# Edge sums in PSUM, biases on DVE, one wide product and a narrower count in a three-sweep graph kernel

## The chip, the cores and the metric

The kernel runs on one core of one Trainium2 chip. The metric is the device time of the whole kernel in microseconds, measured on the chip. Five runs of the kernel before gave 4110.39 us as the median (4082.2 to 4133.68). One further execution was recorded by the hardware profiler and took 4101.04 us; all the rows quoted below are from that execution.

The engines are called PE (TensorE, matrix products), DVE (VectorE, elementwise work), ACT (ScalarE), POOL (GpSimd, which here issues the gathers) and SP (SyncE, which here issues plain transfers). SBUF is the working memory on the chip, PSUM the small memory that PE writes its products to.

## The reference

A graph has 6250 nodes with 256 features each and 100000 edges. Each edge has a source node `src`, a destination node `dst` and 64 features of its own. The edges come sorted by `dst`. Cut to what matters:

```python
# layer 0
theta_x = (x[dst] - x[src]) @ theta_w.T + theta_b
phi_x = x[src] @ phi_w.T + phi_b
x = layernorm(x + segment_max(relu(theta_x + phi_x), dst))   # 0 for a node without edges
# layer 1
hv = x @ W_in + b_in
for W, b in ((W_u0, b_u0), (W_u1, b_u1)):
    m = relu(concatenate([hv[src], edge_attr_64]) @ W + b)
    hv = where(has_in, segment_max(m, dst) + hv, hv)
out = layernorm(x + relu(hv @ W_ro + b_ro))
```

`segment_max` takes, for every node, the maximum over the edges that end in it. Three times, then, a row of 256 numbers is fetched for every edge, something is added, and a maximum is taken over all edges with the same destination.

## The kernel before, in words

**Edges.** The sorted edges lie in 17 blocks (`BLOCKS`: twelve of 56 steps, then 48, 32, 16, 8 and 6; 782 steps, `FS`). In a block each of the 128 partitions holds a contiguous run of edges, and one step handles one edge of every partition. Eight steps are a chunk (`K`), so there are 98 chunks (`NG`).

**Three sweeps** (`sweep(r)`) go over all the steps, each with its own table of node rows in HBM. The product of the node's row is computed once per node, not per edge, and written to `table[r]`. In a sweep:

- POOL gathers the rows of the step's 128 sources into the chunk's tile `run` (`sources`, L719, one indirect DMA a step, issued 16 steps ahead in the order of the program; `run` has four buffers of eight steps).
- In sweeps 1 and 2 the edge's own 64 features add a product. PE multiplies the features of two steps at once with `whe` (`pair`, L730, one 512-column product in a PSUM tile `hp`; two buffers, issued one pair ahead) and DVE adds it to two steps of `run` (L923). `features` loads the features by ACT's queue.
- DVE then takes the running maximum (L926): the new row against the previous step's row, which a per-partition limit `lim` lets through only where the destination is the same.
- After each chunk SP writes the eight rows to `S` in HBM (L932).
- At the end of a block `over_lanes` carries the maximum on from partition to partition: transposes on PE, scans on DVE, copies on ACT.

**Nodes.** The 6250 nodes are 49 tiles of 128. As soon as the blocks of a tile's edges are done, `node` gathers the last row of each node's run from `S` (L771), merges what was carried between partitions (`picks`, `carried`, a product `v`), finishes the node's row and multiplies it for the next sweep. The helper `turned` transposes on PE and copies on ACT (L694); the helper `times` (L697 to L703) multiplies by a weight, two products of 256 columns, and then adds the bias by a third product of a row of ones with the bias row (L702). In sweep 0 these are: theta on `xT` (`theta`, with ACT's copy `theta_out`, L801), and two products of the normalised row, one with a bias for `table[1]` (`first_f`, copied by `first_h`, L830) and one without for `h_sb` (`first_g`, copied by `first_i`, L834). In sweep 1 it is the product for `table[2]` (`next_c`, copied by `next_d`, L849), in sweep 2 the last product, which DVE takes together with the relu and the residual (`last_d`, L853).

**Counting.** In sweep 0 the edges of every node are counted, which yields the position of each node's last edge. Every three steps (slots 4 to 295) `count` compares, on DVE, the low seven bits of the destinations with 0 to 127 (`ol`, L647, 1024 elements for eight steps) and the high bits with 0 to 48 (`oh`, L650, 392 elements), and PE multiplies the two into the histogram `hist` (L653). No node can be finished before the counting ends, which is at step 300.

**Order.** The whole of it is under a manual schedule: each engine executes its instructions in the order in which the Python code emits them. `at(slot, f)` puts a piece of a node's work after the edge work of step `slot`, so the pieces of several nodes interleave with the steps: for a node whose first piece stands at slot b, `picks` at b-3, `carried` at b-2, then `first_a` to `first_i` at b to b+10 (`next_a` to `next_d` at b to b+5, `last_g` at b+9). Theta of tile t is at slot 8t+20 and its copy one slot later. Semaphores between the engines are set from the data dependencies, and a tile with few buffers makes its next writer wait for its last reader.

[...]

**Start.** `fuse` multiplies weights once so that `wcat` holds `W_in` beside `W_in W_u0`, and `fuse_b` folds `b_in` into the other biases, all of which are rows on one partition (`line`).

Of the kernel before, what the change touches and what calls it, by code (L numbers as in the profile page):

```python
# [23 lines left out]
K = 8  # L24
# [525 lines left out]
def in_order(ctx: ExitStack, tc: tile.TileContext, g):  # L550
# [30 lines left out]
    def line(v, name):  # L581
        t = one.tile([1, D], F32, name=name)
        nc.scalar.dma_start(t, v.rearrange("(o f) -> o f", o=1))
        return t
# [47 lines left out]
    def fuse_b():  # L632
        for b, w in ((b2, wu0), (bu1, wu1), (bro, wro)):
            ps = psum.tile([P, 512], F32, tag="pr", name="fuse_p")
            for k in range(2):
                nc.tensor.matmul(ps[:1, :D], binT[:, k:k + 1], w[:, k, :], start=(k == 0), stop=(k == 1))
            nc.vector.tensor_add(b, b, ps[:1, :D])
# [3 lines left out]
    hist = psum.tile([P, 512], F32, tag="v", name="hist")  # L641

    def count(c):
        k = min(K, FS - c * K)
        cut = slice(c * K, c * K + k)
        ol = work.tile([P, K, P], BF16, name="ol", bufs=1)
        nc.vector.tensor_tensor(ol[:, :k, :], col.unsqueeze(1).to_broadcast([P, k, P]),  # L647
                                lo[:, cut].unsqueeze(2).to_broadcast([P, k, P]), OP.is_equal)
        oh = work.tile([P, K, NT], BF16, name="oh", bufs=1)
        nc.vector.tensor_tensor(oh[:, :k, :], col[:, :NT].unsqueeze(1).to_broadcast([P, k, NT]),  # L650
                                hi[:, cut].unsqueeze(2).to_broadcast([P, k, NT]), OP.is_equal)
        for j in range(k):
            nc.tensor.matmul(hist[:, :NT], ol[:, j, :], oh[:, j, :], start=(c == 0 and j == 0),  # L653
# [43 lines left out]
    def times(aT, w, b, n, tag="pr"):  # L697
        ps = psum.tile([P, 512], F32, tag=tag, name="prod")
        for k in range(2):
            nc.tensor.matmul(ps[:, :n], aT[:, k, :], w[:, k, :], start=(k == 0), stop=(k == 1 and b is None))  # L700
        if b is not None:
            nc.tensor.matmul(ps[:, :n], every[0:1, :], b, start=False, stop=True)  # L702
        return ps  # L703

    def sweep(r):
# [21 lines left out]
        def pair(i):  # L727
            c, q = divmod(i, K // 2)
            hp[i] = psum.tile([P, 512], F32, tag="he", name="hp")
# [33 lines left out]
        def node(t, g, b):  # L763
# [22 lines left out]
            def carried():  # L786
                assert max(carried_in) - SPAN[t][0] < KEPT
                o["v"] = psum.tile([P, 512], F32, tag="v", name="v")
# [8 lines left out]
            def theta():  # L797
                o["h"] = times(o["xT"], th, tb, D, tag="he")

            def theta_out():  # L800
                nc.scalar.copy(h_sb[:, t, :], o["h"][:, :D])  # L801
# [20 lines left out]
            def first_f():  # L822
                o["g"] = times(o["aT"], wcat[:, :, D:], b2, D)

            def first_g():
                o["ps"] = times(o["aT"], wcat[:, :, :D], None, D)

            def first_h():
                new = work.tile([P, D], F32, name="new", bufs=3)
                nc.scalar.copy(new, o["g"][:, :D])  # L830
                nc.scalar.dma_start(table[1][t * P:(t + 1) * P, :], new)

            def first_i():
# [158 lines left out]
```

## Time and profile before

| | |
|---|---|
| median of 5 runs | 4110.39 us |
| the profiled execution | 4101.04 us, span 4099.2 us, 22048 instructions |
| granted TensorE clock, mean | 0.664 |
| PE busy | 2040.3 us (50%), 4957 matmuls |
| DVE busy | 2082.8 us (51%) |
| POOL busy | 2462.5 us (60%), 2499 instructions |
| ACT busy | 280.6 us (7%) |
| HBM traffic | 179 GB/s over the span |

The span falls into these stages (busy time of the engines in each, from the profile's windows):

| stage | us | PE | DVE | POOL | granted clock |
|---|---|---|---|---|---|
| sweep 0, counting (130 to 520) | 390 | 163 | 279 | 308 | 0.50 |
| sweep 0, rest of the steps (520 to 1338) | 818 | 294 | 318 | 495 | 0.55 |
| sweep 0, last nodes (1338 to 1392) | 54 | 43 | 31 | 6 | 0.84 |
| sweep 1, steps (1392 to 2675) | 1283 | 680 | 657 | 800 | 0.72 |
| sweep 1, last nodes (2675 to 2724) | 49 | 34 | 19 | 6 | 0.88 |
| sweep 2, steps (2724 to 4019) | 1295 | 706 | 701 | 797 | 0.71 |
| sweep 2, last nodes (4019 to 4099) | 80 | 59 | 41 | 7 | 0.65 |

How to read the rows of the profile: a group's row has the line of the code, the engine, the operation, what is written `<-` what is read, the count, the busy time in us and the mean in ns of one, and after the second bar the engine's idle time just before these instructions with what ended most of it. A product of two f32 operands shows as two matmul rows. The ends of matmuls are modelled in the profile, so that a matmul's result can be later than its row says; when the next instruction that needs it starts is measured. A timeline row has the start in us, the duration in us, the engine, the line and the operation, and in brackets the idle time before it and what ended that.

### The profile page before, as it was taken

Reading aid. Unit: us, or ns where it says so; the run is one execution under the profiler, and the core shown is the slowest. Engines: PE = TensorE matmul, PEld = TensorE weight load, DVE = VectorE, ACT = ScalarE, POOL = GpSimd, SP = SyncE. Lnnn points to the kernel's source line nnn. Section 1 sums busy time; section 2 is a strip of 40 time slices with the busy share of each in tenths; the row PEclk is TensorE's granted clock in tenths of the full one; section 3 lists DMA queues with packets and bytes.
Section 4 is the critical chain, followed back from the end, with each engine's and each line's share of the span. In section 5 each row is a group of like instructions: output and inputs, shape, how many; then the busy total and the mean of one; then the engine's idle time right before and its main releaser. Section 6 shows DMA issues by size and latency. Waiting matters only on the chain.

```text
span 4099.2 us, 22048 instructions
## 1 busy us (share of the span) xinstructions
PE 2040.3 (50%) x4957; PEld 916.1 (22%) x4957; DVE 2082.8 (51%) x4526; ACT 280.6 (7%) x770; POOL 2462.5 (60%) x2499
## 2 busy tenths in 40 slices
PE   5434344232324744455555555664545555455567
PEld 4222222111212311111121222231111212122224
DVE  2776633443334554464554444555556555555555
ACT  1000010000011100000000000110000000000001
POOL 3677755666664466566666655546666666565552
PEclk7555565555556866676677777886667777676766
DMA  6755545554554455565555555545656555454542
GB/s 223 242 190 192 196 155 171 171 176 162 171 168 143 148 190 195 170 216 179 192 194 181 181 178 177 176 154 192 205 178 213 193 183 192 161 190 154 174 161 94
DMA packets 237763, 735.87 MB, mean 180 GB/s; under 512 B 51880, under 2 KB 91799, under 8 KB 200375
## 3 DMA queue, kind: packets, MB, share of 16 engines
q0 software_dynamic: 119664, 326.92, 27.3%
q1 hardware_dynamic: 66096, 334.71, 21.3%
q10 hardware_dynamic: 51862, 72.75, 5.3%
q8 instruction: 42, 0.69, 0.1%
q14 instruction: 99, 0.80, 0.1%
HBM read 401.01 MB, written 333.16 MB: 179 GB/s over the span
## 4 chain that ended last, share of the span: by engine, by line
another core or an unknown queue 29%; issue 18%; PE 16%; DVE 15%; DMA 10%; POOL 10%; ACT 2%; ACTq 0%; POOLq 0%; DVEq 0%; SPq 0%
POOL run L719 9%; DMA run<-table,s_s 7%; DVE run L926 7%; DVE run L923 5%; PE hp L730 5%; PE prod L700 4%; PE prod L702 2%; PE v L790 2%; DMA S<-run 2%; PE ps L533 1%; PE tp L692 1%; POOL m L771 1%; ACT aT L694 1%; DVE oh L650 1%
## 5 line engine op out<-in xcount | busy, mean ns | idle before, releaser
L719 POOL DMA_INDIRECT run<-table,s_s x2346 | 2318.6, 988 | 1295.3 <-issue 658.8
L730 PE MATMUL hp<-whe,hT 128*128 128x512 f32 x1564 | 1058.1, 781 | 594.6 <-DVE run L923 374.3
L926 DVE SCALAR_TENSOR_TENSOR run<-run,lim 128x256 f32<-128x256 f32 x2295 | 1111.1, 484 | 241.4 <-DMA run<-table,s_s 157.9
L923 DVE TENSOR_TENSOR run<-run,hp 128x512 f32<-128x512 f32 x782 | 533.7, 682 | 844.7 <-remote 495.4
L730 PEld LDWEIGHTS hp<-whe,hT 128*128 128x128 f32 x1564 | 307.0, 233 | 1200.5 <-DVE run L923 704.2
L771 POOL DMA_INDIRECT m<-S,end_i x147 | 143.3, 975 | 297.1 <-DMA S<-run 197.1
L700 PE MATMUL prod<-wcat,aT 128*128 128x256 f32 x392 | 162.1, 555 | 267.3 <-ACT aT L694 170.7
L790 PE MATMUL v<-cs,pick 128*128 128x256 f32 (+1 forms) x468 | 197.4, 552 | 125.4 <-DVE pick L783 66.7
L692 PE MATMUL tp<-ident,h_sb 128*128 128x128 f32 x196 | 53.4, 365 | 382.8 <-DVE h_sb L841 255.6
L653 PE MATMUL hist<-oh,ol 128*128 128x49 bf16 x782 | 48.9, 217 | 251.2 <-DVE oh L650 218.4
L700 PEld LDWEIGHTS prod<-wcat,aT 128*128 128x128 f32 x392 | 96.3, 270 | 320.7 <-ACT aT L694 180.9
L790 PEld LDWEIGHTS v<-cs,pick 128*128 128x128 f32 x468 | 119.0, 279 | 203.1 <-DVE pick L783 65.6
L746 DVE TENSOR_TENSOR_SCAN cT<-lim,cT,lp 128x128 f32<-128x128 f32 x96 | 40.8, 467 | 184.6 <-PE lp L741 117.5
L692 PEld LDWEIGHTS tp<-ident,h_sb 128*128 128x128 f32 x196 | 25.2, 174 | 475.5 <-issue 317.4
L700 PE MATMUL prod<-wro,aT 128*128 128x256 f32 x196 | 85.4, 580 | 89.8 <-issue 49.4
L853 DVE SCALAR_TENSOR_TENSOR m<-prod,x_sb 128x256 f32<-128x256 f32 x49 | 20.8, 424 | 210.0 <-remote 96.7
L647 DVE TENSOR_TENSOR ol<-col,lo 128x1024 bf16<-128x1024 bf16 x98 | 119.1, 1215 | 5.6 <-remote 5.5
L837 DVE TENSOR_TENSOR m<-m,v 128x256 f32<-128x256 f32 x98 | 40.5, 413 | 155.6 <-remote 64.2
L700 PE MATMUL prod<-wu,aT 128*128 128x256 f32 x196 | 75.0, 520 | 71.7 <-issue 50.8
L653 PEld LDWEIGHTS <-ol 128*128 128x128 bf16 x782 | 42.7, 117 | 278.3 <-DVE ol L647 179.4
L741 PE MATMUL lp<-ident,run 128*128 128x128 f32 x102 | 28.5, 373 | 152.1 <-ACT lim L739 76.4
L700 PE MATMUL prod<-th,xT 128*128 128x256 f32 x196 | 97.8, 653 | 3.7 <-issue 3.7
(116 smaller groups left out, 1325.0 us busy)
## 6 DMA issues: line engine op xcount, KB each, us to landing
S<-run SPq DMA_DIRECT2D x291, 1024.0 KB
hT<-in_heT ACTq DMA_DIRECT2D x196, 256.0 KB
run<-table,s_s POOLq DMA_INDIRECT x2346
table<-new ACTq DMA_DIRECT2D x98, 128.0 KB
xg<-in_xTn SPq DMA_DIRECT2D x7, 896.0 KB
table<-g SPq DMA_DIRECT2D x7, 896.0 KB
xT<-in_xTn SPq DMA_DIRECT2D x49, 128.0 KB
x_sb<-in_xn SPq DMA_DIRECT2D x7, 896.0 KB
```

Source lines behind the costliest of these rows:

```text
L533: nc.tensor.matmul(ps[:, q * D:(q + 1) * D], xg[:, k, (i + q) * P:(i + q + 1) * P], wd[:, k, :], start=(k == 0), stop=(k == 1))
L647: nc.vector.tensor_tensor(ol[:, :k, :], col.unsqueeze(1).to_broadcast([P, k, P]), lo[:, cut].unsqueeze(2).to_broadcast([P, k, P]), OP.is_e ...
L653: nc.tensor.matmul(hist[:, :NT], ol[:, j, :], oh[:, j, :], start=(c == 0 and j == 0), stop=(c == NG - 1 and j == k - 1))
L692: nc.tensor.transpose(tp[:, k * P:(k + 1) * P], a[:, k * P:(k + 1) * P], ident)
L700: nc.tensor.matmul(ps[:, :n], aT[:, k, :], w[:, k, :], start=(k == 0), stop=(k == 1 and b is None))
L702: nc.tensor.matmul(ps[:, :n], every[0:1, :], b, start=False, stop=True)
L719: nc.gpsimd.indirect_dma_start(out=runs[s // K][:, s % K, :], out_offset=None, in_=table[r], in_offset=bass.IndirectOffsetOnAxis(ap=s_s[:, ...
L730: nc.tensor.matmul(hp[i], hT[c][:, q, :], whe[r - 1].rearrange("p s f -> p (s f)"), start=True, stop=True)
L771: i = nc.gpsimd.indirect_dma_start(out=o["m"], out_offset=None, in_=S_r[:P * (FIRST[SPAN[t][1]] + BLOCKS[SPAN[t][1]]), :], in_offset=bass. ...
L790: nc.tensor.matmul(o["v"][:, :N1], p, cs[:, blk % KEPT, :N1], start=(blk == SPAN[t][0]), stop=(blk == SPAN[t][1]))
L923: nc.vector.tensor_add(two, two, hp.pop(s // 2))
L926: nc.vector.scalar_tensor_tensor(cur, prev, lim[:, s:s + 1], cur, OP.min, OP.max)
```

## The change

Four things are changed together.

1. **Edge rows are summed in PSUM.** In sweeps 1 and 2 DVE adds two steps of `run` into the `hp` tile and leaves the sum there; the running maximum reads the row from PSUM and writes `run`. At the first step of a block, where no maximum is taken, a copy moves the row to `run`. `hp` has three buffers, and `pair` is issued two pairs ahead. In sweep 0 the maximum works on `run` as before.
2. **DVE adds the biases.** `times` has no bias product any more. The bias rows are loaded to all 128 partitions, and `fuse_b` works on all partitions. `theta_out`, `first_g`, `next_d` and `last_d` add the bias on DVE as they copy the product out of PSUM; the first three were copies on ACT, and `last_d` becomes two instructions.
3. **The wide product of pass 0 in one.** The products for `table[1]` and for `h_sb` become one of 512 columns, taken out by `first_g` at slot b+9.
4. **Counting.** ACT copies the low bits to two PSUM tiles (`low`), and `ol` is computed from there; `oh` covers only the node tiles that the chunk's block can contain. A product with zeros clears `hist` first.

The tag `he` has three buffers for these purposes, and `v` with `hist` one.

```diff
     def line(v, name):
-        t = one.tile([1, D], F32, name=name)
-        nc.scalar.dma_start(t, v.rearrange("(o f) -> o f", o=1))
+        t = one.tile([P, D], F32, name=name)
+        nc.scalar.dma_start(t, v.rearrange("(o f) -> o f", o=1).to_broadcast([P, D]))
...
-                nc.tensor.matmul(ps[:1, :D], binT[:, k:k + 1], w[:, k, :], start=(k == 0), stop=(k == 1))
-            nc.vector.tensor_add(b, b, ps[:1, :D])
+                nc.tensor.matmul(ps[:, :D], binT[:, k:k + 1].to_broadcast([P, P]), w[:, k, :], start=(k == 0),
+                                 stop=(k == 1))
+            nc.vector.tensor_add(b, b, ps[:, :D])
...
-    hist = psum.tile([P, 512], F32, tag="v", name="hist")
+    hist = psum.tile([P, 512], F32, tag="v", name="hist", bufs=1)
+
+    none = one.tile([P, NT], BF16, name="none")
+    nc.vector.memset(none, 0.0)
+    half = (NG + 1) // 2
+    low = []
+    for i in range(2):
+        low.append(psum.tile([P, 512], F32, tag="he", name="low", bufs=3))
+        n = min(half * K, FS - i * half * K)
+        nc.scalar.copy(low[i][:, :n], lo[:, i * half * K:i * half * K + n])
 
     def count(c):
...
-                                lo[:, cut].unsqueeze(2).to_broadcast([P, k, P]), OP.is_equal)
+                                low[c // half][:, c % half * K:c % half * K + k].unsqueeze(2).to_broadcast([P, k, P]), OP.is_equal)
+        b = max(i for i in range(NB) if FIRST[i] <= c * K)
+        tiles = [t for t in range(NT) if SPAN[t][0] <= b <= SPAN[t][1]]
+        t0, w = tiles[0], len(tiles)
         oh = work.tile([P, K, NT], BF16, name="oh", bufs=1)
-        nc.vector.tensor_tensor(oh[:, :k, :], col[:, :NT].unsqueeze(1).to_broadcast([P, k, NT]),
-                                hi[:, cut].unsqueeze(2).to_broadcast([P, k, NT]), OP.is_equal)
+        nc.vector.tensor_tensor(oh[:, :k, :w], col[:, t0:t0 + w].unsqueeze(1).to_broadcast([P, k, w]),
+                                hi[:, c * K:c * K + k].unsqueeze(2).to_broadcast([P, k, w]), OP.is_equal)
+        if c == 0:
+            nc.tensor.matmul(hist[:, :NT], ol[:, 0, :], none, start=True, stop=False)
         for j in range(k):
-            nc.tensor.matmul(hist[:, :NT], ol[:, j, :], oh[:, j, :], start=(c == 0 and j == 0),
+            nc.tensor.matmul(hist[:, t0:t0 + w], ol[:, j, :], oh[:, j, :w], start=False,
                              stop=(c == NG - 1 and j == k - 1))
...
-            nc.tensor.matmul(ps[:, :n], aT[:, k, :], w[:, k, :], start=(k == 0), stop=(k == 1 and b is None))
-        if b is not None:
-            nc.tensor.matmul(ps[:, :n], every[0:1, :], b, start=False, stop=True)
+            nc.tensor.matmul(ps[:, :n], aT[:, k, :], w[:, k, :], start=(k == 0), stop=(k == 1))
...
-            hp[i] = psum.tile([P, 512], F32, tag="he", name="hp")
+            hp[i] = psum.tile([P, 512], F32, tag="he", name="hp", bufs=3)
...
-                o["v"] = psum.tile([P, 512], F32, tag="v", name="v")
+                o["v"] = psum.tile([P, 512], F32, tag="v", name="v", bufs=1)
...
             def theta_out():
-                nc.scalar.copy(h_sb[:, t, :], o["h"][:, :D])
+                nc.vector.tensor_add(h_sb[:, t, :], o["h"][:, :D], tb)
...
             def first_f():
-                o["g"] = times(o["aT"], wcat[:, :, D:], b2, D)
+                o["ps"] = times(o["aT"], wcat, 2 * D)
 
             def first_g():
-                o["ps"] = times(o["aT"], wcat[:, :, :D], None, D)
-
-            def first_h():
                 new = work.tile([P, D], F32, name="new", bufs=3)
-                nc.scalar.copy(new, o["g"][:, :D])
+                nc.vector.tensor_add(new, o["ps"][:, D:], b2)
                 nc.scalar.dma_start(table[1][t * P:(t + 1) * P, :], new)
-
-            def first_i():
                 nc.scalar.copy(h_sb[:, t, :], o["ps"][:, :D])
...
             def next_d():
                 new = work.tile([P, D], F32, name="new", bufs=3)
-                nc.scalar.copy(new, o["ps"][:, :D])
+                nc.vector.tensor_add(new, o["ps"][:, :D], bu1)
...
             def last_d():
-                nc.vector.scalar_tensor_tensor(o["m"], o["ps"][:, :D], 0.0, x_sb[:, t, :], OP.max, OP.add)
+                nc.vector.tensor_add(o["m"], o["ps"][:, :D], bro)
+                nc.vector.scalar_tensor_tensor(o["m"], o["m"], 0.0, x_sb[:, t, :], OP.max, OP.add)
...
-                             (8, first_g), (9, first_h), (10, first_i)):
+                             (9, first_g)):
...
+                    pair(1)
...
-                if s % 2 == 0:
-                    if s + 2 < FS:
-                        pair(s // 2 + 1)
-                    two = runs[c][:, j:j + 2, :].rearrange("p s f -> p (s f)")
-                    nc.vector.tensor_add(two, two, hp.pop(s // 2))
+            if s % 2 == 0:
+                two = runs[c][:, j:j + 2, :].rearrange("p s f -> p (s f)")
+                if r > 0:
+                    if s + 4 < FS:
+                        pair(s // 2 + 2)
+                    sums = hp.pop(s // 2)
+                    nc.vector.tensor_add(sums, sums, two)
+                else:
+                    sums = two
             cur = runs[c][:, j, :]
+            row = sums[:, s % 2 * D:(s % 2 + 1) * D]
             if s > FIRST[blk]:
-                nc.vector.scalar_tensor_tensor(cur, prev, lim[:, s:s + 1], cur, OP.min, OP.max)
+                nc.vector.scalar_tensor_tensor(cur, prev, lim[:, s:s + 1], row, OP.min, OP.max)
+            elif r > 0:
+                nc.vector.tensor_copy(cur, row)
```

More of the change, by code (lines that the diff above doesn't have):

```diff
@@ L643, in count @@
+    none = one.tile([P, NT], BF16, name="none")
[6 more added lines that the diff above has]
+        nc.scalar.copy(low[i][:, :n], lo[:, i * half * K:i * half * K + n])
     def count(c):
         k = min(K, FS - c * K)
-        cut = slice(c * K, c * K + k)
         ol = work.tile([P, K, P], BF16, name="ol", bufs=1)
         nc.vector.tensor_tensor(ol[:, :k, :], col.unsqueeze(1).to_broadcast([P, k, P]),
-                                lo[:, cut].unsqueeze(2).to_broadcast([P, k, P]), OP.is_equal)
+                                low[c // half][:, c % half * K:c % half * K + k].unsqueeze(2).to_broadcast([P, k, P]), OP.is_equal)
+        b = max(i for i in range(NB) if FIRST[i] <= c * K)
+        tiles = [t for t in range(NT) if SPAN[t][0] <= b <= SPAN[t][1]]
+        t0, w = tiles[0], len(tiles)
@@ L695, in turned, with times @@
         return aT
-    def times(aT, w, b, n, tag="pr"):
-        ps = psum.tile([P, 512], F32, tag=tag, name="prod")
+    def times(aT, w, n, tag="pr"):
+        ps = psum.tile([P, 512], F32, tag=tag, name="prod", bufs=3 if tag == "he" else 2)
         for k in range(2):
-            nc.tensor.matmul(ps[:, :n], aT[:, k, :], w[:, k, :], start=(k == 0), stop=(k == 1 and b is None))
-        if b is not None:
-            nc.tensor.matmul(ps[:, :n], every[0:1, :], b, start=False, stop=True)
+            nc.tensor.matmul(ps[:, :n], aT[:, k, :], w[:, k, :], start=(k == 0), stop=(k == 1))
         return ps
@@ L797, in theta @@
             def theta():
-                o["h"] = times(o["xT"], th, tb, D, tag="he")
+                o["h"] = times(o["xT"], th, D, tag="he")
             def theta_out():
-                nc.scalar.copy(h_sb[:, t, :], o["h"][:, :D])
+                nc.vector.tensor_add(h_sb[:, t, :], o["h"][:, :D], tb)
             def first_a():
@@ L844, in next_c @@
             def next_c():
-                o["ps"] = times(o["aT"], wu1 if r == 1 else wro, bu1 if r == 1 else bro, D)
+                o["ps"] = times(o["aT"], wu1 if r == 1 else wro, D)
             def next_d():
                 new = work.tile([P, D], F32, name="new", bufs=3)
-                nc.scalar.copy(new, o["ps"][:, :D])
+                nc.vector.tensor_add(new, o["ps"][:, :D], bu1)
                 nc.scalar.dma_start(table[2][t * P:(t + 1) * P, :], new)
             def last_d():
-                nc.vector.scalar_tensor_tensor(o["m"], o["ps"][:, :D], 0.0, x_sb[:, t, :], OP.max, OP.add)
+                nc.vector.tensor_add(o["m"], o["ps"][:, :D], bro)
+                nc.vector.scalar_tensor_tensor(o["m"], o["m"], 0.0, x_sb[:, t, :], OP.max, OP.add)
             def last_e():
```

## The prediction

> **What bounds the kernel now.** I read the chain that ended last first, because the busy shares (PE 50%, DVE 51%, POOL 60%) name no engine.
>
> ```profile
> another core or an unknown queue 29%; issue 18%; PE 16%; DVE 15%; DMA 10%; POOL 10%; ACT 2%; ACTq 0%; POOLq 0%; DVEq 0%; SPq 0%
> ```
>
> On one core, 29% for "an unknown queue" means waits whose releaser the profile did not find. The costliest groups say where they sit:
>
> ```profile
> L719 POOL DMA_INDIRECT run<-table,s_s x2346 | 2318.6, 988 | 1295.3 <-issue 658.8
> L730 PE MATMUL hp<-whe,hT 128*128 128x512 f32 x1564 | 1058.1, 781 | 594.6 <-DVE run L923 374.3
> L926 DVE SCALAR_TENSOR_TENSOR run<-run,lim 128x256 f32<-128x256 f32 x2295 | 1111.1, 484 | 241.4 <-DMA run<-table,s_s 157.9
> L923 DVE TENSOR_TENSOR run<-run,hp 128x512 f32<-128x512 f32 x782 | 533.7, 682 | 844.7 <-remote 495.4
> ```
>
> The edge sum L923 idles 845 us, mostly on "remote". The timeline shows on what: a stretch at 1442 us, then one at 1512 us.
>
> ```profile
> 1441.62 0.69 DVE L923 TENSOR_TENSOR run<-run,hp 128x512 f32<-128x512 f32 x1 [3.88 <-remote]
> 1442.36 2.08 PE L730 MATMUL hp<-whe,hT 128*128 128x512 f32 x2 [3.53 <-issue]
> 1447.21 0.69 DVE L923 TENSOR_TENSOR run<-run,hp 128x512 f32<-128x512 f32 x1 [3.86 <-remote]
> 1447.95 2.07 PE L730 MATMUL hp<-whe,hT 128*128 128x512 f32 x2 [3.51 <-DVE run L923]
> ...
> 1512.39 1.12 PE L730 MATMUL hp<-whe,hT 128*128 128x512 f32 x2 [0.53 <-DVE run L923]
> 1513.29 0.68 DVE L923 TENSOR_TENSOR run<-run,hp 128x512 f32<-128x512 f32 x1
> 1514.03 1.12 PE L730 MATMUL hp<-whe,hT 128*128 128x512 f32 x2 [0.51 <-DVE run L923]
> 1514.93 0.68 DVE L923 TENSOR_TENSOR run<-run,hp 128x512 f32<-128x512 f32 x1
> ```
>
> At 1512 us (granted clock 1.0) a pair of steps takes 1.64 us: 0.68 for the sum and 2 x 0.48 for the maxima, DVE back to back. At 1442 us (clock 0.5) it takes 5.6 us; the matmul is drawn as 2.08 us, but its semaphore, which DVE waits for, comes 5.6 us after the one before. PE crawls there, whatever its row says. POOL starts a gather every 1.25 us, so a pair costs it 2.5 us. While PE crawls POOL gets ahead until its four run buffers are full, and stands still; then PE recovers and DVE catches up. I added POOL's idle stretches over 1 us: 199, 258 and 287 us in the three sweeps of about 1332, 1332 and 1376 us. **The time is POOL's 831 gathers a sweep (about 1050 us) plus what PE makes it stand still, plus a tail.**
>
> One stage differs: the counting, 130 to 520 us, where POOL never stops but is itself slow.
>
> ```profile
> 300.06 1.22 DVE L647 TENSOR_TENSOR ol<-col,lo 128x1024 bf16<-128x1024 bf16 x1
> 300.73 1.36 POOL L719 DMA_INDIRECT run<-table,s_s  x1 [0.30 <-issue]
> 301.19 0.56 DVE L650 TENSOR_TENSOR oh<-col,hi 128x392 bf16<-128x392 bf16 x1
> 302.40 1.09 POOL L719 DMA_INDIRECT run<-table,s_s  x1 [0.30 <-issue]
> ```
>
> Gathers that run beside L647 take 1.27 us on the mean, with DVE idle 0.945. Start to start it is 1.448 us over the stage's 269 gathers and 1.271 us in the rest of sweep 0.
>
> **The change, part by part**, against the profiled execution: 4101.0 us, span 4099.2, 9 us under the median of 4110.4.
>
> *Counting.* `ol` keeps one SBUF input; `oh` shrinks from 392 elements to 8 times a few tiles, some 40: 0.19 us by the 0.17 us of the 17-element L617, for 0.56. If the second SBUF input is what holds POOL up, its step falls to the 1.28 us of the rest of the sweep, where L926 still has two: 269 x 0.17 = **-45 us**. Bounds: 0, if it is not the input, and 269 x (1.448 - 1.25) = -53. Next late would be DVE: per 8 steps 2.67 x (1.22 + 0.19) + 8 x 0.52 + 0.41 for the moved theta add = 8.3 us, plus a wait for theta's product. In that stage the ACT copy followed its step's maximum by 2.2 to 3.2 us; without the bias's 1.07 us that is 1.1 to 2.1, in one of three cases under other DVE work, so 1.25 on average: 9.6 us against POOL's 10.2. Hidden, with 0.6 us to spare.
>
> [...]
>
> *Edge sums in PSUM.* The sum writes where it read; the maximum reads a PSUM row. Rows: L806, a maximum with a PSUM input and a pointer scalar, takes 484 ns, as L926 does now; 0. Bounds 1530 x (424 - 484) = -92 us of DVE by L853 (an immediate scalar), and +92 the other way; DVE is 51% busy, so little of either shows. 34 copies at block starts, 0.4 us each, lie beside POOL. One SBUF input less on these 1530 maxima: the 1562 gathers of sweeps 1 and 2 average 0.97 against 0.945 us, so at most 1562 x 0.025 = -39; I take **-25**. The third `hp` buffer lets PE run two pairs ahead, but a crawling PE is short of speed, not of work: bounds 0 and the 118 us that L923 waits for PE by name; I take **-10**.
>
> [...]
>
> *Bias matmuls gone.* 196 products lose one; each is two rows of 128x256. At 618 us six such rows (`wcat`, then `b`) kept the consumer waiting from 618.04 to 626.71, 1.44 us a row; drawn rows are 0.5 to 0.7. In sweep 0 a node has some 21 rows (4 + 2 for theta, 8 + 2 for the wide product, 3 for `v`, the rest transposes), of which 4 go: 19% of the 184 us that POOL stood still after the counting (199 less 15 at 110 us): **-35**, and -5 in the tail. In sweeps 1 and 2, 98 of some 2100 rows of 256 columns go in each, 4.6%. Pairs over 3.4 us hold 1552 of the 2573 us of these sweeps; 4.6% of that is 71 us of crawling, of which between a third (the part in which POOL stood still) and all counts: 24 to 71, taken **-40**. The bounds for all bias terms: 0, if POOL's stalls have another cause, and -120.
>
> *Wide product of pass 0.* Four rows of 512 columns for eight of 256: the same columns, 4 weight loads less, overlapped: 0, bounds ±10.
>
> *Work moved from ACT to DVE*: 147 adds of 0.41 us, 49 more in `last_d`: 80 us, in DVE's idle half: **+10**. The price is in the order: theta_out, first_g and next_d now make DVE wait for PE, with the chain of maxima behind them, and POOL waits for that through the run buffers; `table<-new` on ACT's queue then waits for DVE. Sweep 2 already has this wait (L853, 210 us idle) and its 782 steps took 1295 us against 1283 in sweep 1, so in sweep 1 at most 12, taken **+5**. In sweep 0 after the counting 13 theta adds and 49 first_g are in question:
>
> ```profile
> 623.06 1.91 PE L700 MATMUL prod<-th,xT 128*128 128x256 f32 x4
> ...
> 647.71 0.37 ACT L801 COPY h_sb<-prod 128x256 f32<-128x256 f32 x1 [20.63 <-remote]
> ...
> 649.16 0.16 DVE L805 TENSOR_SCALAR no<-v 128x1 f32<-128x1 f32 x1 [32.58 <-remote]
> ```
>
> Here theta's consumer was 24 us late, but DVE stood on the same PE queue until 649 anyway. I take **+15**; bounds 0 and the 200 us of the first rival.
>
> *Start and single buffers.* fuse_b loads 128 columns for 1, six bias lines become 128 rows each, and DVE already waits there 32 us for L637: **+5**, bounds 0 and +15. `v` keeps one buffer: the next node's matmul waits for this node's first_a, which comes two steps earlier in the order while `hp` holds PE as tightly; 0, up to +20 in the tails.
>
> Sum: -45 - 25 - 10 - 35 - 5 - 40 + 10 + 5 + 15 + 5 = -125; 4101 - 125 = 3976, said as **3980 us**, 3% below the median shown. [...]
>
> **Rivals.** *DVE becomes the place where everything waits* (slower). ACT idled 258 us before L830 and, by the timeline, some 143 us between step and L801 after the counting. If half of these 400 us becomes waiting that DVE did not have, 200 us, less the -45, -25 and -25 of counting, ports and half the bias: 4101 + 105 = 4205. It decides once an added wait outlasts POOL's lead, some 24 steps or 30 us, or if PE also crawls in the counting. For it: theta sits one step before its consumer. Against: L853 in sweep 2. *The ports do not matter*: the -45 and -25 fail, PE's gains are eaten by the waits: about 4090, no change. *PE stops crawling*: with less node work and two pairs queued, half of POOL's 545 us of idling in sweeps 1 and 2 goes as well: about 3710. Against: in a crawl PE already has two pairs queued.
>
> **Numbers.** Forecast (3880 to 4065) 0.60, larger gain 0.10, no change 0.13, slower 0.17. About 1% either way is what a measurement of this kernel can tell from no change. Faster 0.70, same 0.13, slower 0.17. The range takes most of the slower rival and part of the larger gain: 3800 to 4190.
>
> **What would show it.** Gathers in the counting start 1.25 to 1.3 us apart, not 1.45; those beside L926 fall to 0.95 us in sweeps 1 and 2 and not in sweep 0. Maxima stay near 0.48 us. The bias rows (202 us of PE by L702) are gone, POOL's idle sum falls from 744 to about 650 us. I am wrong if DVE's waits for `prod` in sweep 0 push POOL's idling past 200 us, or if crawling takes another share of the time than now: nothing in the profile fixes that share.

## The result, and the profile after

The changed kernel takes 4092.5 us (median of 42 runs, 4054.5 to 4133.4) against 4101.3 us for the kernel before (79 runs, 4055.9 to 4146.5). The ratio, which leaves out the runs more than 1.5% above the fastest of their kernel, is 0.9987, with a 95% interval of 0.9972 to 1.0002: no change that a measurement can tell. Its profiled execution took 4080.6 us, with a span of 4078.5.

The work did shrink where the change cuts it. GpSimd's (POOL) busy time fell from 2462.5 to 2381.9 us and TensorE's (PE) from 2040 to 1788.5. The time of a sweep is taken here from its first gather to the first gather of the next one, of sweep 2 to the end; "standing still" is the sum of the gaps over 1 us between two gathers of the sweep, those from `S` for the node tiles included; a "step" is the mean from one start of a gather to the next, over the gathers that follow within 2.2 us. In the counting, "time lost" is what 240 steps took beyond 240 times the mean step.

| | before | after |
|---|---|---|
| sweep 0: time, standing still | 1332, 199 us | **1373, 290 us** |
| sweep 1: time, step, standing still | 1332, 1.275, 258 us | 1306, 1.253, 253 us |
| sweep 2: time, step, standing still | 1376, 1.273, 287 us | 1340, 1.252, 281 us |
| gather for step 300 issued (end of the counting) | 505.1 us | **562.4 us** |
| counting, steps 60 to 300: step, time lost beside it | 1.450, 1 us | **1.286, 96 us** |

Sweeps 1 and 2 gained 61 us together in these two executions. The profiled executions of two later runs, `theta_act` and `bits_sbuf`, have the same code in these sweeps and make it 42 and 28, so the gain is real but smaller than one pair of profiles says. Sweep 0 lost 40, and it lost them in the counting, the stage from which the forecast took its largest term. There the step fell as forecast, and yet the stage got longer, since GpSimd now stops ten times in it.

The page of the changed kernel, its chain and its costliest groups (busy us, mean ns of one | idle before, and what ended most of it):

```profile
issue 25%; DVE 24%; another core or an unknown queue 22%; PE 13%; POOL 7%; DMA 5%; ACT 1%; ACTq 0%; DVEq 0%; POOLq 0%; SPq 0%
...
L731 POOL DMA_INDIRECT run<-table,s_s x2346 | 2240.2, 955 | 1368.6 <-issue 715.6
...
L934 DVE TENSOR_TENSOR hp<-hp,run 128x512 f32<-128x512 f32 x782 | 543.2, 695 | 487.6 <-remote 218.9
L940 DVE SCALAR_TENSOR_TENSOR run<-run,lim,hp 128x256 f32<-128x256 f32 x1530 | 733.2, 479 | 46.5 <-issue 0.2
...
L940 DVE SCALAR_TENSOR_TENSOR run<-run,lim 128x256 f32<-128x256 f32 x765 | 369.4, 483 | 153.6 <-issue 63.8
...
L656 DVE TENSOR_TENSOR ol<-col,low 128x1024 bf16<-128x1024 bf16 x98 | 118.9, 1213 | 150.8 <-remote 149.3
```

A gather is 955 ns for 988, and a maximum with a PSUM row costs 479 ns, no more than the SBUF form's 483. The chain still names no engine; "an unknown queue" is now 22%. The granted clock does not tell the kernels apart: its mean is 0.673 for 0.664 before. The last row is the new one: the compare `ol` idled 5.6 us in the kernel before and 150.8 now. Its waits in the stage, VectorE (DVE) only (engine, line, waited for: us in all, times, longest), first in the kernel before from 60 to 500 us, then in the changed one from 60 to 560 us:

```profile
DVE ol L647 <- remote: 5.5, 4, 2.5
```

```profile
DVE ol L656 <- remote: 134.7, 20, 14.4
```

What it waits for shows in the timeline of the changed kernel (start us, us, engine, line, operation, [idle before, released by]):

```profile
167.28 1.52 DVE L940 SCALAR_TENSOR_TENSOR run<-run,lim 128x256 f32<-128x256 f32 x3
...
167.43 0.35 PE L667 MATMUL hist<-oh,ol 128*128 128x3 bf16 x8 [3.75 <-DVE oh L662]
...
173.67 0.95 POOL L731 DMA_INDIRECT run<-table,s_s  x1 [0.30 <-issue]
174.92 0.94 POOL L731 DMA_INDIRECT run<-table,s_s  x1 [0.30 <-issue]
176.08 1.22 DVE L656 TENSOR_TENSOR ol<-col,low 128x1024 bf16<-128x1024 bf16 x1 [7.29 <-remote]
```

`ol` has one buffer, so the next compare waits until the eight tiny products of the last one have read it. By their rows these end at 167.8; the compare starts at 176.08, 8.3 us later, while POOL issues a gather every 1.25 us and gets ahead. At 183.6 it has run out of buffers and stands still for 14 us.

### The profile page after: what moved, and what is told of

Read it like the earlier page. It is cut to its first block, busy times and chain, and to the rows that moved or that the text cites. A ratio compares the mean times of both kernels' runs of the same rounds, so it can differ in the third digit from the quotient of the medians.

```text
span 4078.5 us, 21055 instructions
## 1 busy us (share of the span) xinstructions
PE 1788.5 (44%) x4370; PEld 763.3 (19%) x4370; DVE 2128.1 (52%) x4757; ACT 229.6 (6%) x625; POOL 2381.9 (58%) x2499
## 3 DMA queue, kind: packets, MB, share of 16 engines
q0 software_dynamic: 119664, 326.92, 27.5%
## 4 chain that ended last, share of the span: by engine, by line
issue 25%; DVE 24%; another core or an unknown queue 22%; PE 13%; POOL 7%; DMA 5%; ACT 1%; ACTq 0%; DVEq 0%; POOLq 0%; SPq 0%
DVE run L940 11%; DVE hp L934 8%; POOL run L731 6%; PE hp L742 5%; PE prod L714 5%; DMA run<-table,s_s 4%; PE v L802 1%; PE tp L706 1%; DMA S<-run 1%; DVE st L692 1%; DVE pick L795 1%; POOL m L783 1%; ACT aT L708 1%; DVE ol L656 0%
## 5 line engine op out<-in xcount | busy, mean ns | idle before, releaser
L731 POOL DMA_INDIRECT run<-table,s_s x2346 | 2240.2, 955 | 1368.6 <-issue 715.6
L934 DVE TENSOR_TENSOR hp<-hp,run 128x512 f32<-128x512 f32 x782 | 543.2, 695 | 487.6 <-remote 218.9
L940 DVE SCALAR_TENSOR_TENSOR run<-run,lim,hp 128x256 f32<-128x256 f32 x1530 | 733.2, 479 | 46.5 <-issue 0.2
L940 DVE SCALAR_TENSOR_TENSOR run<-run,lim 128x256 f32<-128x256 f32 x765 | 369.4, 483 | 153.6 <-issue 63.8
L656 DVE TENSOR_TENSOR ol<-col,low 128x1024 bf16<-128x1024 bf16 x98 | 118.9, 1213 | 150.8 <-remote 149.3
L667 PE MATMUL hist<-oh,ol 128*128 128x4 bf16 (+7 forms) x782 | 34.8, 167 | 366.2 <-DVE oh L662 257.2
L714 PE MATMUL prod<-wcat,aT 128*128 128x512 f32 x196 | 150.5, 911 | 43.1 <-issue 24.8
L706 PE MATMUL tp<-ident,x_sb 128*128 128x128 f32 x98 | 28.1, 381 | 296.5 <-DVE x_sb L701 136.5
L860 DVE TENSOR_TENSOR m<-prod,bro 128x256 f32<-128x256 f32 x49 | 20.8, 424 | 214.2 <-remote 109.6
L839 DVE TENSOR_TENSOR new<-prod,b 128x256 f32<-128x256 f32 x49 | 20.8, 424 | 170.8 <-remote 84.7
```

The lines of the kernel that those rows point to most:

```text
L667: nc.tensor.matmul(hist[:, t0:t0 + w], ol[:, j, :], oh[:, j, :w], start=False, stop=(c == NG - 1 and j == k - 1))
L706: nc.tensor.transpose(tp[:, k * P:(k + 1) * P], a[:, k * P:(k + 1) * P], ident)
L731: nc.gpsimd.indirect_dma_start(out=runs[s // K][:, s % K, :], out_offset=None, in_=table[r], in_offset=bass.IndirectOffsetOnAxis(ap=s_s[:, ...
L934: nc.vector.tensor_add(sums, sums, two)
L940: nc.vector.scalar_tensor_tensor(cur, prev, lim[:, s:s + 1], row, OP.min, OP.max)
```

## The experiments

Two theories at the start. **A**: the bias of theta, now added by VectorE, makes it wait for a product every eight steps. **B**: the change freed GpSimd; with gathers every 1.25 us TensorE serves its products slowly (the "crawl" of the prediction), and in the counting of the kernel before only the slow compare, which held GpSimd at 1.45 us, had kept that away.

### Parts undone, and one part alone

`theta_act`, the bias of theta back on TensorE and ScalarE:

```
-                o["h"] = times(o["xT"], th, D, tag="he")
+                (two matmuls with th, then)
+                nc.tensor.matmul(ps[:, :D], every[0:1, :], tb[0:1, :], start=False, stop=True)
...
-                nc.vector.tensor_add(h_sb[:, t, :], o["h"][:, :D], tb)
+                nc.scalar.copy(h_sb[:, t, :], o["h"][:, :D])
```

> The changed kernel with one part undone: the bias of theta goes back into PSUM with a third matmul and ScalarE copies the rows, so VectorE waits for no theta product during the counting. Theory A (VectorE's wait for theta, each eight steps, is what made the counting longer): the gather for step 300 is issued at about 460 to 480 us instead of 562, first sweep near 1290, total near 4010. Theory B (the counting got longer because GpSimd, freed by the PSUM read, runs at 1.25 us a step and TensorE then crawls): step 300 stays at 550 to 580, since the counting matrices still come from a crawling TensorE; total 4070 to 4110.

Ratio to the kernel before 0.9932 (0.9902 to 0.9962), 4096.1 us. Step 300 at 577.0 us, 118 us lost in the counting, sweep 0 1388 us. Theory A falls: the counting is as long without theta's wait.

`bits_sbuf`, the low bits read from SBUF again:

```
-                                low[c // half][:, c % half * K:c % half * K + k].unsqueeze(2)...
+                                lo[:, c * K:c * K + k].unsqueeze(2)...
```

> The changed kernel with one part undone: the counting reads the low bits from SBUF again, so that its compare has two SBUF inputs; all else, the bias of theta on VectorE too, is as changed. Theory A (theta's wait): step 300 stays at 560 or later, total 4090 or more. Theory B (GpSimd's speed sets off the crawl of TensorE): gathers beside the compare slow to about 1.27 us again, a step takes 1.4 to 1.45 us, GpSimd does not stand still between 125 and 500 us, and step 300 is issued near 505; total near 4035, faster than both kernels.

0.9895 (0.9855 to 0.9935), 4082.2 us: a part of the change taken back makes it faster. The step in the counting is 1.374 us, since the narrow `oh` stays, so only half of the way to 1.450; 50 us are lost instead of 96, step 300 comes at 535.0. Not the 505 of theory B, but in its direction and, as the table below shows, on its line.

`count_alone`, the counting part put into the kernel before:

```
-        cut = slice(c * K, c * K + k)
...
-                                lo[:, cut].unsqueeze(2).to_broadcast([P, k, P]), OP.is_equal)
+                                low[c // half][:, c % half * K:c % half * K + k].unsqueeze(2)...
+        (oh and hist over the block's tiles only; hist and v one buffer, "he" three)
```

> The kernel before with the counting part of the change alone (low bits in PSUM, high bits over only the tiles of the block, and the buffers that this takes); biases and edge sums as before. Theory A: with theta's bias on TensorE and its copy on ScalarE the counting gains what was forecast, step 300 near 460 instead of 505, total near 4060. Theory B: step 300 at 550 or later instead of 505, total near 4150.

1.0100 (1.0067 to 1.0133), 4162.5 us. Step 300 at 556.1, 93 us lost, sweep 0 1380 us for 1332; sweeps 1 and 2 as before (1339, 1367). The counting part alone makes the kernel slower, by 1.0% or some 40 us; the rest of the change gives that back.

### GpSimd held back on purpose

`paced`, a fill of a scratch tile on GpSimd ahead of each gather, 64 columns in sweep 1 and 256 in sweep 2:

```
         def sources(s):
+            if r > 0:
+                nc.gpsimd.memset(pause[:, :(0, 64, 256)[r]], 0.0)
```

> The changed kernel with a fill of 64 columns on GpSimd ahead of every gather of the second sweep and of 256 columns in the third: GpSimd's step is made longer on purpose, the first sweep is as changed (1373). Theory B (TensorE crawls when GpSimd runs unhindered, and GpSimd's standing still is paid for it): a step of 1.35 to 1.45 us, with much less standing still (253 and 281 us in the changed kernel, under 120 here); a sweep that loses nothing on balance, 1220 to 1310. Theory A (crawl is not tied to GpSimd's rate): the added time comes on top where GpSimd runs, standing still falls by less than half of it, sweeps of 1350 to 1450.

0.9718 (0.9668 to 0.9767), 4015.6 us. Sweep 2 with a step of 1.437 us: standing still 25 us, time 1246 for 1340. Sweep 1 with 1.338: 246 us, 1322. Where a fill stands between two gathers, the gap includes it; GpSimd's idle time alone is 191 us in this sweep 1 and 23 in sweep 2. More work on GpSimd, less time in sweep 2; the 64 columns of sweep 1 gain nothing, against the expectation. What VectorE's sum waits for in sweep 2, in the changed kernel (from 2760 to 4000 us), and below in the paced one (from 2785 us on):

```profile
DVE hp L934 <- remote: 89.6, 27, 4.6
...
DVE hp L934 <- PE hp L742: 39.3, 14, 3.5
...
DVE hp L934 <- DMA run<-table,s_s: 20.4, 11, 4.6
```

```profile
DVE hp L939 <- DMA run<-table,s_s: 302.7, 184, 5.4
...
DVE hp L939 <- PE hp L747: 13.8, 7, 7.1
```

In the paced kernel the sum waits 13.8 us for products and 302.7 us for rows, as it should when GpSimd sets the pace.

`paced_all` has 256 columns in all sweeps, `before_paced` the same fill in the kernel before:

```
+            w = (256, 256, 256)[r]
+            if w:
+                nc.gpsimd.memset(pause[:, :w], 0.0)
```

> The changed kernel with the fill of 256 columns ahead of every gather of all three sweeps. Theory B: no sweep has crawling pairs; step 300 of the first sweep is issued near 500 (60 + 300 x 1.44 + some 10) although theta's bias stays on VectorE, the first sweep takes 1230 to 1260 instead of 1373, the second 1220 to 1250 instead of 1306, the third 1246 as in the last run; total near 3790. If the counting had its own cause (theta's wait), step 300 stays at 550 or later, the first sweep at 1310 or more, total near 3860.

> The kernel before with the same fill of 256 columns ahead of every gather of all sweeps. It shows what the change is worth once TensorE does not crawl. If the change is worth nothing but GpSimd's time (a gather of 970 against 947 ns beside the edge sums, 2346 gathers): some 50 slower than the paced changed kernel, near 3840. If the crawl was only tied to the changed kernel's parts: the kernel before gains nothing, 4100 or more.

`paced_all`: 0.9195 (0.9141 to 0.9249), 3775.1 us; sweeps 1254, 1225 and 1237, standing still 4, 9 and 10 us; step 300 at 503.3 us with theta's bias still on VectorE. `before_paced`: 0.9431 (0.9375 to 0.9487), 3867.9 us. So the kernel before suffered from the same thing, and without it the change is worth 93 us by the medians, 75 by the profiled spans (3773.7 against 3848.8). The page of `paced_all`:

```profile
POOL 69%; issue 13%; DMA 7%; DVE 6%; PE 3%; ACT 0%; POOLq 0%; DVEq 0%; ACTq 0%
POOL run L736 49%; POOL pause L733 17%; DMA run<-table,s_s 7%; POOL m L788 3%; DVE hp L939 2%; DVE run L945 2%; PE prod L714 2%; PE v L807 0%; PE tp L706 0%; DVE ol L656 0%; PE hp L747 0%; ACT aT L708 0%; POOLq L736 0%; DMA hT<-in_heT 0%; DVE h_sb L853 0%
...
L736 POOL DMA_INDIRECT run<-table,s_s x2346 | 2267.8, 967 | 483.9 <-issue 405.0
...
L939 DVE TENSOR_TENSOR hp<-hp,run 128x512 f32<-128x512 f32 x782 | 548.2, 701 | 837.2 <-DMA run<-table,s_s 789.5
...
L656 DVE TENSOR_TENSOR ol<-col,low 128x1024 bf16<-128x1024 bf16 x98 | 118.6, 1211 | 0.0
```

Now the chain names its engine: GpSimd 69%, the "unknown queue" is gone, and `ol` never waits. The granted clock is no rival: in the counting (130 to 500 us) it is 0.50 in the changed kernel and in `paced_all` alike, over the whole span 0.673 and 0.677.

`paced_sums_sbuf` puts the sums of the paced kernel back into SBUF:

```
-                    nc.vector.tensor_add(sums, sums, two)
-                else:
-                    sums = two
+                    nc.vector.tensor_add(two, two, sums)
+                sums = two
...
-            elif r > 0:
-                nc.vector.tensor_copy(cur, row)
```

> The paced changed kernel (256 columns) with the sums of the edge rows back in SBUF, so that sum and maximum have two SBUF inputs again; counting and biases as changed. If the two-input operations slow GpSimd (a gather and its fill 1.467 against 1.439 us a step in the two paced kernels, whose end GpSimd sets): second and third sweep 22 us longer each, total near 3820. If the sums' place is worth nothing and the gap between the paced kernels lies in the biases: second and third sweep at 1225 and 1237, total near 3775.

0.9249 (0.9202 to 0.9297), 3811.8 us: 37 us for the place of the sums alone. The step in sweeps 1 and 2 is 1.463 and 1.467 for 1.439 and 1.441, and the gathers' group shows it against the 967 ns above:

```profile
L736 POOL DMA_INDIRECT run<-table,s_s x2346 | 2307.3, 984 | 483.5 <-issue 402.8 <-DMA tb<-in_theta_b 36.6 <-DMA hT<-in_heT 32.0
```

With the sums in SBUF the maximum reads two rows in SBUF, and a gather takes a little longer: 984 against 967 ns.

### Where the bound lies

`pace_map` has 128, 128 and 384 columns in the three sweeps, `pace192` and `pace224` what they are called in all of them; the diff is the width.

> The changed kernel with fills of 128 columns in the first and second sweep and of 384 in the third: steps of about 1.37 and 1.50 us. Theory B with a threshold between 1.34 us (a fill of 64, which still crawled) and 1.44 us (256, which did not): the third sweep is bound by GpSimd alone, 782 x 0.065 = 50 us longer than with 256, near 1295; the second lies between 1210 (free of the crawl: 1246 less 782 x 0.07, and less a shorter tail) and 1320. If pacing only trades standing still for pause, the second is near 1320 and the third near 1250.

> The changed kernel with a fill of 192 columns ahead of every gather, between 128 (a step of 1.37 us, GpSimd still stood still for 129 and 167 us a sweep) and 256 (1.44 us, 4 to 10 us). If the bound between the two lies above 1.40 us: stops come back, 3790 to 3880. If it lies below: GpSimd alone sets the end, 2346 x 0.035 = 80 us shorter than with 256, near 3695.

> The changed kernel with a fill of 224 columns ahead of every gather, a step of 1.42 us between 1.40 (GpSimd stood still for 73 to 128 us a sweep) and 1.44 (4 to 10 us). If the bound lies at 1.40 to 1.41: no standing still, 2346 x 0.018 = 42 us shorter than with 256, near 3733. If it lies above 1.42: some standing still, 3780 to 3850.

`pace_map` took 3952.7 us in one run; `pace192` 0.9515 (0.9453 to 0.9576), 3929.5 us, longer than either expectation; `pace224` 0.9163 (0.9111 to 0.9215), 3762.3 us, between its two. With what was measured before, for sweep 1:

| columns of the fill | step, us | standing still, us | sweep 1, us |
|---|---|---|---|
| none (after) | 1.253 | 253 | 1306 |
| 64 | 1.338 | 246 | 1322 |
| 128 | 1.364 | 167 | 1287 |
| 192 | 1.399 | 128 | 1294 |
| 224 | 1.412 | 36 | 1225 |
| 256 | 1.439 | 9 | 1225 |
| 384 (sweep 2) | 1.544 | 10 | 1319 |

With the fill taken out of the gaps, GpSimd's idle time is 191, 138, 117, 35 and 8 us for 64 to 256 columns: it falls all along, and most between 192 and 224 columns. Below about 1.41 us a step the stops cost more than the shorter fill saves (1294 us at 1.399, 1225 at 1.412); from 1.44 on each hundredth of a step costs 8 us a sweep (sweep 2: 1237 us at 1.441, 1319 at 1.544). The counting lies on the same line without any fill: 1.276 to 1.287 us and 93 to 118 us lost, 1.374 and 50, 1.450 and 1. The fills of 224 and 256 columns are not told apart by their intervals; both beat the two kernels by 8%.

### What is slow: products, bytes or signals

`no_pair` leaves out the products of the edge features in sweeps 1 and 2, not paced:

```
-                    pair(0)
-                    pair(1)
...
-                    if s + 4 < FS:
-                        pair(s // 2 + 2)
-                    sums = hp.pop(s // 2)
-                    nc.vector.tensor_add(sums, sums, two)
+                    sums = three[1 + s // 2 % 2]
+                    nc.vector.tensor_add(sums, three[0], two)
```

> The changed kernel, not paced, with the products of the edge features left out in the second and third sweep: VectorE adds a PSUM buffer of zeros to the gathered rows at the same cost, the features are still loaded, and TensorE has only the node rows and the lane step. If GpSimd's standing still comes of VectorE waiting for slow pair products: it falls from 253 and 281 us to under 100, and the sweeps to 1080 to 1180. If GpSimd at 1.25 us a step stands still for its own buffers and the landing of S, whatever TensorE does: 200 us or more, sweeps of 1250 to 1330.

4034.6 us in one run. Standing still is 229 and 245 us, the sweeps 1282 and 1309: 782 products gone, and only 23 and 31 us with them (at most 45 a sweep against the profiled executions of `theta_act` and `bits_sbuf`). So GpSimd also stops when there are no pair products to wait for. The numbers are those of the second case, its own buffers, but VectorE, which has to empty these, is not on time either: its waits have moved to a place that should have none. Sweep 2 of this kernel, VectorE's waits:

```profile
DVE run L938 <- remote: 209.7, 79, 6.5
DVE run L938 <- issue: 88.1, 45, 6.5
DVE run L938 <- DVE run L938: 46.4, 66, 0.9
DVE run L938 <- DVE hp L932: 30.1, 32, 1.3
```

L938 is the maximum. Its operands name one signal, the one that VectorE's own instruction before it gives. A stretch of the timeline, from sweep 1 (POOL's and SP's rows left out):

```profile
1573.31 0.69 DVE L932 TENSOR_TENSOR hp<-hp,run 128x512 f32<-128x512 f32 x1
...
1575.71 0.48 DVE L938 SCALAR_TENSOR_TENSOR run<-run,lim,hp 128x256 f32<-128x256 f32 x1 [1.71 <-issue]
...
1577.11 0.48 DVE L938 SCALAR_TENSOR_TENSOR run<-run,lim,hp 128x256 f32<-128x256 f32 x1 [0.92 <-DVE run L938]
1577.51 0.69 DVE L932 TENSOR_TENSOR hp<-hp,run 128x512 f32<-128x512 f32 x1
...
1579.91 0.48 DVE L938 SCALAR_TENSOR_TENSOR run<-run,lim,hp 128x256 f32<-128x256 f32 x1 [1.71 <-remote]
1581.31 0.48 DVE L938 SCALAR_TENSOR_TENSOR run<-run,lim,hp 128x256 f32<-128x256 f32 x1 [0.92 <-DVE run L938]
...
1583.41 0.48 DVE L938 SCALAR_TENSOR_TENSOR run<-run,lim,hp 128x256 f32<-128x256 f32 x1 [1.01 <-DVE hp L932]
```

VectorE stands 1.71 us after its own sum and 0.92 us after its own maximum; undisturbed (1587 to 1610 us) these gaps are 0.03 us. All these starts of the maximum lie on a grid of 0.70 us: 1575.71, 1577.11, 1579.91, 1581.31, 1583.41 are 2, 4, 2 and 3 times 0.70 apart. TensorE has no row between 1537 and 1610 us. By these rows what is late is the signal between two instructions, not the work of either: the sum ends at 1574.00 us, the maximum that needs it starts at 1575.71.

`half_rows` halves the bytes of the gathers of sweeps 1 and 2, not paced:

```
-                out=runs[s // K][:, s % K, :], out_offset=None, in_=table[r],
+                out=runs[s // K][:, s % K, :H], out_offset=None,
+                in_=table[r] if r == 0 else table[r].rearrange("n (h f) -> (n h) f", h=2),
...
```

> The changed kernel, not paced, in whose second and third sweep a gather fetches 128 columns a row instead of 256 (half the bytes, and the wrong half rows; VectorE reads them twice, at the same cost), with as many gathers and descriptors. If the bytes gathered set off the crawl of TensorE: the pairs come on time, GpSimd's standing still falls to under 100 us, sweeps of 1080 to 1180. If the pace of the gathers itself does: standing still stays at 200 us or more, sweeps of 1270 to 1340.

4121.9 us in one run; standing still 282 and 289 us, sweeps 1335 and 1349. Half the bytes bring no gain.

`paced_traffic` and `paced_signals` add copies to sweep 2 of the paced kernel, the first one of 256 KB each eight steps, the second 128 pieces of 256 bytes each step:

```
+                nc.scalar.dma_start(spill[c], heT[c])
```

```
+                nc.scalar.dma_start(spill[c, :, j * 64:(j + 1) * 64], heT[c, :, j * 64:(j + 1) * 64])
```

> As the paced changed kernel in all sweeps, and in the third sweep each block of features is copied once more, from device memory to device memory (256 KB each eight steps, about 22 GB/s read and as much written, more than the pause takes off the gathers' and the rows' traffic). If the crawl of TensorE comes of the amount of DMA traffic, the third sweep crawls again: GpSimd stands still for over 150 us, 1300 or more. If it comes of how fast GpSimd issues gathers, or of what TensorE itself is asked for, the third sweep stays within 1240 to 1265 and GpSimd stands still for under 60 us.

> As the paced changed kernel (256 columns), and in the third sweep one more small copy a step from device memory to device memory, in 128 pieces of 256 bytes, as many pieces as a gather has rows, issued from ScalarE's queue. If completions and packets of any DMA make the signals late, the third sweep falls back to standing still over 100 us and 1290 or more. If only what GpSimd itself issues counts, it stays within 1235 to 1260 with under 40 us.

With large copies sweep 2 takes 1240 us and stands still for 15, though the DMA engines moved 223 GB/s there for 202. With small ones it takes 1290 and stands still for 68: between the two expectations, nearer the first. VectorE's waits are back there, 50.1 us of its sum for "remote" and 37.1 for `hp` (8.0 in `paced_all`):

```profile
DVE hp L941 <- remote: 50.1, 26, 6.1
...
DVE m L865 <- PE hp L747: 41.8, 8, 7.7
DVE hp L941 <- PE hp L747: 37.1, 23, 2.9
```

Both copies add the same 25.7 MB; the large ones add some 3000 DMA packets to the 238486 of the paced kernel, the small ones some 113000, and 782 copies instead of 98. So the number of pieces or of completions counts here, the bytes do not; which of the two is not told apart. Against the pieces speaks `half_rows`: there the packets of the gathers' queue fell with the bytes, from 119664 to 94640, and the stops stayed.

`pace_burst` lets seven gathers follow each other at full speed and breaks once in eight steps:

```
+            if s % K == K - 1:
+                for _ in range(3):
+                    nc.gpsimd.memset(pause, 0.0)
```

> The changed kernel with three fills of 384 columns after every eighth gather instead of one of 256 ahead of each: seven gathers follow each other at 1.25 us, then there is a break of some 1.5 us, on the mean about 1.44 us a step. If something with a queue serves a gather in about 1.40 us and signals stand in that queue: eight steps put it behind by 8 x 0.15 = 1.2 us at most and the break clears it; no standing still, 3760 to 3800. If every pair of gathers closer than 1.40 us makes signals late: standing still as in the changed kernel, over 150 us a sweep, 4000 or more.

0.9298 (0.9249 to 0.9348), 3814.8 us, the profiled execution 3787.9. Beyond the breaks GpSimd stands still for 19, 65 and some 70 us, against 290, 253 and 281; step 300 is issued at 502.9. So gathers 1.255 us apart did little harm here with a break every eight steps. That fits the queue of the expectation, which no run shows, but not cleanly: sweeps 1 and 2 keep 65 and 70 us of standing still, the time lies above the 3760 to 3800 that was expected, and the even pace is better by 40 us.

## Why the prediction was wrong

**The step that failed is the counting, -45.** Its first half held: the step went from 1.450 to 1.286 us (1.28 was forecast), and with the second SBUF input put back it is 1.374 (`bits_sbuf`). Its second half, "Next late would be DVE: ... Hidden, with 0.6 us to spare", took the signals to come as promptly as in a stage with a step of 1.45 us. At 1.286 they did not; 96 us are lost where there was 1, and the stage ends 57 us later. The part alone costs some 40 us (`count_alone`). From -45 to +40 or +57 is 85 to 102 us, most of the 116 by which the sum of -125 missed the -9 of the medians; the rest lies in sweeps 1 and 2. The prediction's own condition, "I am wrong if DVE's waits for `prod` in sweep 0 push POOL's idling past 200 us", was met (290), but by the compare's wait for `hist`: `prod` had little part, as `theta_act` shows.

**Under it lies a wrong reading: "PE crawls there, whatever its row says."** The wait was for a signal from TensorE, so I took TensorE to be slow. `no_pair` shows such lateness with TensorE idle (no row between 1537 and 1610 us) and VectorE waiting 0.92 to 1.71 us for itself there, so a slow TensorE is not needed for it; that in the changed kernel, too, the signal and not the product is late is argued from this, not shown. In the counting the row of the products ended at 167.8 us and the compare that waits for them started at 176.08, 8.3 us later; these two rows fit a late signal and a slow product alike, and only a consumer that depends on no product tells them apart.

The other terms:
- *Second SBUF input of the maxima ("ports" in the prediction), -25.* Right in kind, somewhat small: 37 us in the paced kernels. Without the fill a shorter step was paid back in standing still: in sweep 1 the step is 1.253 us for 1.439 with 256 columns, and standing still 253 us for 9.
- *Bias matmuls -40 and third buffer -10 in sweeps 1 and 2.* With the -25 above and the +5 for the order the forecast for these sweeps was -70; -61 came by the one pair of profiles, -42 and -28 by the two others. The reason was not shown: 782 products less of TensorE were worth only 23 and 31 us, and in the paced kernels counting and biases together, without the sums, are worth 38 us by the profiled spans, 25 of them in sweep 0 (56 us by the medians, from two rounds of measurement).
- *Sweep 0 after the counting, -35 for the bias products and +15 for the order.* From step 300 to the first gather of sweep 1 it took 870 us for 887: -17 where -20 was forecast. This part of the sum held.
- *Bias of theta on VectorE, part of +15.* Its ratio in `theta_act`, 0.9932, lies under the changed kernel's 0.9987, while its profiled sweep 0 is longer by 16 us; the profiled execution is the slowest of its six. Not settled.
- *A maximum with a PSUM row, 0.* Right: 479 against 483 ns.

**The rivals.** The first rival named its condition, "or if PE also crawls in the counting", and waits of that kind came, 134.7 us of `ol` for "remote", at a price of some 40 us instead of 200. It did not carry the kernel to 4205, since sweeps 1 and 2 gained. The time fell into "no change" (about 4090 was named), for a reason that the rival of that name ("the ports do not matter") did not have: the second SBUF input mattered (1.374 against 1.286 us a step in the counting), and so GpSimd crossed the bound of about 1.41 us in one stage more.

**What stays open.** Why the late starts in `no_pair` lie on a grid of 0.70 us, and why a step of about 1.41 us, two of its units, is the bound. A queue shared by the gathers' pieces or completions and the engines' signals would fit the narrow bound (128 us of standing still at 1.399 us a step, 36 at 1.412), the burst and the small copies; that is a guess of mine, and no run shows the queue itself. In `no_pair` signals were still late from 1571 us on, after GpSimd had stood still for 5.7 us, and on time from 1587 us on, after 7.1 us, with gathers 1.25 us apart in both stretches. Nor is it shown why VectorE's own signals are late in `no_pair` but on time in the changed kernel (628.5 against 46.5 us of idling ahead of the 1530 maxima that read `hp`), where it is the sums that wait for TensorE and "remote" (95.1 and 218.9 us). Every execution here was recorded with spans and clock; whether signals are late in one that nothing records, no run here shows.

## What to carry to other kernels

When an engine far ahead of its consumers issues small indirect gathers back to back, try to slow it before speeding anything up: here a useless fill of 224 or 256 columns ahead of each gather took 8% off the changed kernel, more than all the edits of the change. The width has to be measured: 64 columns gained nothing. When a wait ends long after the row that it waits for, look in the same stretch for an instruction that waits for its own engine; if that is late too, as by 1.7 us in `no_pair`, the signals may be slow and not the engine. And when a stage is the only one without stops, ask what makes it so before removing its slowest operation.

## What the runs showed that I had not expected

- Signals from VectorE to itself came 0.9 and 1.7 us late in `no_pair`, on a grid of 0.70 us; in the changed kernel a wait on TensorE ended 8.3 us after its row. Both were seen where gathers of 128 rows start less than about 1.41 us apart on the mean: in sweep 1, standing still is 128 us at 1.399, 36 at 1.412 and 9 at 1.439.
- Half the bytes a gather: no gain (282 and 289 us of standing still for 253 and 281). 21 GB/s more of large copies: next to nothing (15 us for 10). The same bytes in 128 pieces of 256 bytes each step: 68 us.
- With maxima of two SBUF inputs in sweeps 1 and 2 of the paced kernel a gather on GpSimd took longer: 984 against 967 ns over all gathers, 37 us of the whole.
